# A two-layer graph network on one core: halves of x made anew in each pass, a bias moved to VectorE, new durations in the planner, and two bursts summed in a row in layer 2

## The chip, the cores and the metric

The kernel runs on one core of a Trainium2 chip. The metric is the time of one execution on the device in microseconds (us). TensorE multiplies matrices, VectorE and ScalarE work elementwise, GpSimd here issues indirect DMAs (gathers), and SyncE, ScalarE and GpSimd have DMA queues. In the profile these are PE, DVE, ACT, POOL and SP.

## The reference

Cut to what is computed; N = 6250 nodes, E = 100000 edges, sorted by destination, 256 features, 512 hidden.

```python
def _gin_agg(h, src, dst, eps, n_nodes):
    agg = jax.ops.segment_sum(h[src], dst, num_segments=n_nodes)
    return (1.0 + eps) * h + agg
h = _gin_agg(x, src, dst, eps1, n)            # 6250 x 256
h = jax.nn.relu(h @ W1a + b1a)                # 256 -> 512
h = jax.nn.relu(h @ W1b + b1b)                # 512 -> 512, called h1 below
h = _gin_agg(h, src, dst, eps2, n)            # 6250 x 512
h = jax.nn.relu(h @ W2a + b2a)                # 512 -> 512
out = h @ W2b + b2b                           # 512 -> 256
x = _layernorm(x + out)
```

The destinations are the squares of uniform numbers times 6250, so low nodes have many edges and high nodes few.

## The kernel before, in words

Nodes lie in 49 tiles of 128 (the last has 106). Each layer sums the rows of its table (x in layer 1, h1 in layer 2) over the edges in two ways.

**Light edges** go by gathers. An indirect DMA of GpSimd (`gather`, L450) fetches 128 rows, one edge to a partition. Four of them are a burst, kept in one of six pieces of the buffer `early` (layer 2 has `late` beside it). TensorE sums a burst with four selection matrices `sel` (L942; VectorE makes them at L907), whose result is split (L968 in layer 1; L976 and L978 in layer 2), moved to its rows by a second matmul with `to` (L987; made at L912), and added to the tile's accumulator `acc` on VectorE (L997). A layer has 502 gathers in 126 bursts and 59 groups. The gather that reuses a piece waits for the sum that read it six bursts ago.

**Heavy edges**, those of the first 7 tiles, go by count matrices. VectorE compares numbers with the edges' ends (`ca` L1530, `cb` L1538), TensorE multiplies these into counts (L1576), VectorE adds them into `at` (L1599), ScalarE converts a piece of them (`cf`, L1423), and TensorE multiplies counts by x itself (L1466). For that product x is needed as two parts that add up to it, a rounded one and what the rounding left: its halves, in `xh`. The 7 tiles are taken in four passes, (6,5), (4,3), (2,1) and (0), and each pass goes through all 13 ranges of x (12 of four tiles, one of a single short tile). In the first pass a range of x is loaded (`raw`, L1174), ScalarE makes the rounded half (L1381), VectorE subtracts (L1383), and both halves are written to a DRAM tensor `halves`. The other three passes load the halves from there, and ScalarE rounds both again in place (L1403). Layer 2 reads the saved counts back and multiplies them by halves of h1 (`upper` and `xr`, L1205, L1209, products L1313, added at L1256).

**The dense part** (`dense`) takes up to four tiles whose sums are complete: transposes (L1033), the first weights (L1072), bias and relu on ScalarE (L1082), the second weights (L1103). In layer 1 the second bias comes through TensorE: a matmul (L1102) of a constant `twice` with `first_bias`, a tile holding the bias in two rows as a rounded value and the rest, starts each accumulation. ScalarE then takes the relu from PSUM (L1113) and a DMA on its queue writes h1 (L1114). Layer 2 adds x and the bias (L1121, L1122) and normalises. `first_bias` is made at the start by two small DMAs on ScalarE's queue, a copy on ScalarE and a subtraction on VectorE (L715 to L719), between the check of the inputs (L678, the flag on which the program branches) and the branch.

**The order of the work** is written out by a planner (`Plan`) when the program is built: processes ask for an engine with an assumed duration and a priority, for a buffer (`Room`), or for an event, and the planner hands out the engines in simulated time. What it decides is fixed: each engine runs its instructions in that order and waits for semaphores. Gathers are assumed to take 1.255 us each (`GATHER`), and to land `LANDINGS` later. All of h1 has to be written before layer 2's first gather.

## Time and profile before

| | |
|---|---|
| time, median of 3 runs | 1380.43 us (1375.78 to 1381.38) |
| profiled execution | 1377.27 us, span 1375.3 us, clock 0.964 |
| busy: PE, DVE, ACT, POOL | 1239.8, 832.7, 564.5, 986.1 us |
| DMA | 340.61 MB, mean 248 GB/s |
| halves | 36 loads and 12 writes of 1 MB |

The span is the time from the first to the last instruction of the profiled execution; the execution's own time is 2 us longer. Busy shares are means over the start (checks and tables, to about 31 us), layer 1 (gathers to 671 us), the passage to layer 2 (to 694 us), layer 2 (gathers to 1334 us) and its end. A PE that is busy need not be at its peak, since matmuls overlap.

### The profile page before, as it was taken

To read this page: it belongs to the slowest core of one execution; us is meant where nothing else is said; L and a number is where in the kernel's file an instruction comes from. 1 tells how busy PE (TensorE), PEld (TensorE's weight loads), DVE (VectorE), ACT (ScalarE), POOL (GpSimd) and SP (SyncE) were. 2 spreads that over 40 slices of the span, in tenths; PEclk is the share of its full clock that TensorE was granted. 3 is DMA by queue.
4 is the path that set the end of the run, shared out by engine and by line. 5 is a ranking of instruction groups with operands and counts; after the bars stand their busy time and mean duration, and the time that the engine had idled before them with its cause. 6 is when DMAs were issued, how large, how long until landed. Compare 5 with 4: busy or idle time off the path is not lost.

```text
span 1375.3 us, 18780 instructions
## 1 busy us (share of the span) xinstructions
PE 1239.8 (90%) x6120; PEld 740.1 (54%) x6120; DVE 832.7 (61%) x1940; ACT 564.5 (41%) x977; POOL 986.1 (72%) x1018
## 2 busy tenths in 40 slices
PE   2599999798999999969759999999899999999996
PEld 1245455454554555534426666666566666666666
DVE  7587787576676666401127877687666655655343
ACT  0322477446673675472254433333333323333212
POOL 6677777777777777767367777777777777777760
PEclk9799999899999999989979999999999999999999
DMA  4764489868884888597379888888878989888770
GB/s 105 255 215 143 149 301 330 289 188 275 285 271 155 284 263 274 188 367 226 91 268 325 292 268 261 265 299 268 286 246 302 294 272 307 264 298 253 238 218 30
DMA packets 168188, 340.61 MB, mean 248 GB/s; under 512 B 26108, under 2 KB 74836, under 8 KB 168082
## 3 DMA queue, kind: packets, MB, share of 16 engines
q0 software_dynamic: 64256, 197.46, 45.3%
q1 hardware_dynamic: 81554, 116.23, 25.2%
q10 hardware_dynamic: 22272, 25.63, 5.3%
q8 instruction: 52, 0.85, 0.2%
q14 instruction: 54, 0.44, 0.1%
HBM read 295.99 MB, written 43.24 MB: 247 GB/s over the span
## 4 chain that ended last, share of the span: by engine, by line
PE 57%; DMA 17%; POOL 8%; issue 6%; ACT 4%; DVE 4%; ACTq 0%; DVEq 0%; SPq 0%; POOLq 0%
PE bank L1103 15%; PE bank L1072 12%; PE bank L942 9%; PE bank L1313 7%; POOL early L450 5%; PE bank L987 5%; PE bank L1466 4%; DMA early<-h,srcs 4%; PE bank L1576 3%; POOL late L450 3%; DMA late<-h,srcs 3%; DMA acc<-in_x_dram 3%; PE bank L1033 2%; DMA xh<-halves 2%; PE bank L1102 1%
## 5 line engine op out<-in xcount | busy, mean ns | idle before, releaser
L450 POOL DMA_INDIRECT early<-in_x_dram,srcs x502 | 496.1, 988 | 171.6 <-issue 130.7
L450 POOL DMA_INDIRECT early<-h,srcs x250 | 242.4, 970 | 98.6 <-issue 63.4
L450 POOL DMA_INDIRECT late<-h,srcs x252 | 244.9, 972 | 77.4 <-issue 66.4
L997 DVE SCALAR_TENSOR_TENSOR acc<-bank,mask,acc 128x256 f32<-128x256 f32 (+1 forms) x420 | 247.0, 607 | 78.7 <-PE bank L987 77.5
L1103 PE MATMUL bank<-w1b_s,ht 128*128 128x512 f32 (+1 forms) x392 | 193.7, 619 | 0.0
L1072 PE MATMUL bank<-zt,w2a_s 128*128 128x256 f32 (+2 forms) x864 | 181.6, 364 | 2.2 <-ACT zt L1045 2.2
L942 PE MATMUL bank<-early,sel 128*32 128x256 f32 (+1 forms) x1504 | 152.4, 479 | 23.1 <-DMA early<-h,srcs 12.7
L1072 PEld LDWEIGHTS bank<-zt,w2a_s 128*128 128x128 f32 x864 | 151.8, 192 | 37.1 <-issue 8.4
L1599 DVE TENSOR_TENSOR at<-bank,at 128x490 f32 x173 | 116.1, 671 | 83.8 <-PE bank L1576 33.2
L907 DVE TENSOR_TENSOR sel<-iota,slot 128x256 f32<-128x256 f32 (+2 forms) x118 | 51.7, 438 | 171.2 <-PE bank L942 155.0
L1313 PE MATMUL bank<-upper,cf 128*128 128x512 f32 (+1 forms) x343 | 148.6, 433 | 6.0 <-ACT upper L1205 5.1
L987 PE MATMUL bank<-split,to 128*128 128x256 f32 (+3 forms) x360 | 118.6, 430 | 33.4 <-ACT split L976 9.4
L1313 PE MATMUL bank<-xr,cf 128*128 128x512 f32 (+1 forms) x343 | 137.6, 401 | 0.0
L1466 PE MATMUL bank<-xh,cf 128*128 128x512 f32 (+1 forms) x343 | 114.7, 455 | 10.6 <-ACT xh L1403 10.5
L987 PEld LDWEIGHTS bank<-split,to 128*128 128x128 f32 (+1 forms) x360 | 65.3, 197 | 105.2 <-ACT ht L1082 17.6
L1237 ACT CAST cf<-ci 128x512 fp32r<-128x512 uint16 (+1 forms) x91 | 53.8, 595 | 145.6 <-PE bank L1313 108.4
L1103 PEld LDWEIGHTS bank<-w1b_s,ht 128*128 128x128 f32 (+1 forms) x392 | 71.0, 193 | 69.9 <-issue 65.0
L1072 PE MATMUL bank<-zt,w1a_s 128*128 128x256 f32 (+2 forms) x432 | 99.3, 378 | 4.5 <-ACT zt L1045 3.6
L1103 PE MATMUL bank<-w2b_s,ht 128*128 128x256 f32 (+1 forms) x392 | 102.9, 388 | 0.0
L1538 DVE TENSOR_SCALAR cb<-numbers,spot 128x490 f16<-128x490 f16 x280 | 92.5, 361 | 0.0
L1082 ACT ACTIVATE ht<-bank,b2a_s 128x256 f32<-128x256 f32 (+2 forms) x108 | 44.3, 452 | 116.9 <-PE bank L1072 116.8
L1072 PEld LDWEIGHTS bank<-zt,w1a_s 128*128 128x128 f32 x432 | 79.0, 199 | 22.8 <-ACT zt L1045 7.0
(142 smaller groups left out, 1517.9 us busy)
## 6 DMA issues: line engine op xcount, KB each, us to landing
xh<-halves SPq DMA_DIRECT2D x36, 1024.0 KB
halves<-xh SPq DMA_DIRECT2D x12, 1024.0 KB
h<-h1r ACTq DMA_DIRECT2D x48, 256.0 KB
xr<-h SPq DMA_DIRECT2D x12, 1024.0 KB
counts<-ci ACTq DMA_DIRECT2D x84, 128.0 KB
ci<-counts SPq DMA_DIRECT2D x84, 128.0 KB
acc<-h SPq DMA_DIRECT2D x19, 512.0 KB
early<-in_x_dram,srcs POOLq DMA_INDIRECT x502
```

Of the source, the lines that this page charges most:

```text
L450: nc.gpsimd.indirect_dma_start(out=rows_[:, j, :], out_offset=None, in_=table, in_offset=bass.IndirectOffsetOnAxis(ap=srcs[:, c : c + 1], ...
L907: nc.vector.tensor_tensor(sel[:, :n, :], iota[:, :SLOTS].unsqueeze(1).to_broadcast([P, n, SLOTS]), slot[:, c0 : c0 + n].unsqueeze(2).to_br ...
L942: mm = nc.tensor.matmul(pm[b * SLOTS : (b + 1) * SLOTS], sel[:, c - c0, :], rows_[:, j, :], start=(c == parts[b][0]), stop=(c == parts[b][ ...
L987: nc.tensor.matmul(pu[:, i * width : (i + 1) * width], to[:used], split[:used, l, :], start=(once or l == 0), stop=(once or l == 1),)
L997: nc.vector.scalar_tensor_tensor(acc[t], pu[:, i * width : (i + 1) * width], mask[:, t - lo[g], g : g + 1], acc[t], op0=ALU.mult, op1=ALU.add,
L1072: nc.tensor.matmul(ph[:, (f - o) * TILES * P : (f - o) * TILES * P + nb], wa[:, k, f * P : (f + 1) * P], zt[:, k, :nb], start=(k == 0), st ...
L1103: nc.tensor.matmul(po[:m], ht[:, f, i * P : i * P + m], wb[:, f, :], start=(not once and f == 0), stop=(f == KH - 1),)
L1237: nc.scalar.copy(cf_token.tile[:, :n, :].rearrange("p k j -> p (k j)"), token.tile[:, : n * P],)
L1313: nc.tensor.matmul(bank[token.number][:, :width], cf[:m, j, :], of[:m, j, :], start=(j == 0 and of is upper), stop=(j == len(ks) - 1 and o ...
L1466: nc.tensor.matmul(bank[tokens[i].number][:, : 2 * width], cf[:m, j, :], xh[:m, j, :, :].rearrange("p a d -> p (a d)"), start=(k == 0), st ...
L1538: made = nc.vector.tensor_scalar(token.tile, numbers, spot[:, c : c + 1], None, op0=ALU.is_equal)
L1599: nc.vector.tensor_tensor(to, bank[token.number][:, : NT * W].rearrange("p (k w) -> p k w", w=W), to, op=ALU.add,)
```

## The change

1. `first_bias` and `twice` are gone. A DMA spreads the bias over all partitions into `b1b_s`; VectorE adds it to the second product while taking that from PSUM (L1115 of the new file), and ScalarE takes the relu in SBUF (L1117). `h1r` has three buffers instead of two.
2. `halves` is gone. Each pass loads x itself, and ScalarE and VectorE halve it (L1371, L1373): 52 halvings (48 full, 4 short) instead of 13. `xh` has two buffers instead of three, `raw` two instead of one. The loading begins after 80 us of planned time instead of 20.
3. The planner's assumed durations and priorities differ: elementwise work on VectorE and ScalarE is shorter, a burst's sum is 0.2 plus 0.0021 a column, layer 1's landings take 5 us instead of 3, TensorE gets 0.1 us between two jobs in layer 1, and at most four PSUM banks hold counts (`SIDE`). `cb` has ten buffers instead of nine; its comparisons are ordered two by two.
4. Within a pair of groups layer 2 asks for two bursts together and sums them one behind the other (`JOIN`).

```diff
-LANDINGS = (3.0, 6.0)
+LANDINGS = (5.0, 6.0)
-SUMS = 0.0025
+SUMS = 0.0021
+TURN = 0.2
+JOIN = (1, 2)
+SIDE = 4
 def dve(n):
-    return 0.15 + 0.00105 * n
+    return 0.085 + 0.00105 * n
...
-    twice = const.tile([64, P], F32R, name="twice")
-    nc.vector.tensor_copy(twice, ones[:64].to_broadcast([64, P]))
-    first_bias = const.tile([64, H], F32R, name="first_bias")
-    with tc.tile_pool(name="biases", bufs=1) as biases:
-        whole = biases.tile([64, H], F32, name="whole")
-        nc.vector.memset(whole, 0.0)
-        for k in (0, 32):
-            nc.scalar.dma_start(whole[k : k + 1], b1b.rearrange("(o n) -> o n", o=1))
-        nc.scalar.copy(first_bias, whole)
-        nc.vector.tensor_tensor(
-            first_bias[32:33], whole[32:33], first_bias[32:33], op=ALU.subtract
-        )
+    b1b_s = const.tile([P, H], F32, name="b1b_s")
+    nc.scalar.dma_start(b1b_s, b1b.partition_broadcast(P))
...
+                    for j in range(0, len(todo), n):
+                        some = todo[j : j + n]
+                        for i in some:
+                            yield ("until", selected[pieces[number][i][0]])
+                            yield ("until", arrived[i])
+                        shared = shared or (yield ("get", banks, 0))
+                        yield ("on", "PE", TURN + SUMS * width * len(some), 0)
...
-                        if once and not f:
-                            nc.tensor.matmul(po[:m], twice[:, :m], bias, start=True, stop=False)
...
+                            yield ("on", "DVE", dve(H), 1)
+                            h = h_token.tile
+                            nc.vector.tensor_tensor(h[:m], po[:m], bias[:m], op=ALU.add)
                             yield ("on", "ACT", act(H) + 0.1, 1)
-                            nc.scalar.activation(h[:m], po[:m], AF.Relu)
+                            nc.scalar.activation(h[:m], h[:m], AF.Relu)
...
                 def loading():
+                    yield ("rest", 80.0)
                     for ts, r in turns:
-                        if ts is PASSES[0]:
-                            raw = yield ("get", raw_room, 0)
-                            in_rows(ks, raw.tile, table)
+                        raw = yield ("get", raw_room, 0)
+                        in_rows(ranges[r], raw.tile, table)
                         token = yield ("get", xh_room, 0)
-                        if ts is PASSES[0]:
-                            plan.start(halving(ts, r, xh, raw))
-                        else:
-                            yield ("until", stored[r])
-                            in_rows(
-                                ks, xh.bitcast(F32).rearrange("p k a d -> p k (a d)"),
-                                halves.rearrange("n a d -> n (a d)"),
-                            )
-                            plan.start(rounding(ts, r, xh))
+                        xh_of[ts, r] = token
+                        plan.start(halving(ts, r, token.tile, raw))
...
                         tokens = []
                         for i in some:
-                            tokens.append((yield ("get", banks, 2)))
+                            permit = yield ("get", permits, 0)
+                            tokens.append(((yield ("get", banks, 2)), permit))
```

Where instructions stand now, at three places. In the rows, the name ahead of `<-` is what is written, the rest what is read.

VectorE, near the end of layer 1, before: selection matrices, additions of sums, and the last counts; the halves of this pass come from DRAM.

```order
L1599 TENSOR_TENSOR at<-bank_496,at 128x49x10
L997 SCALAR_TENSOR_TENSOR acc<-bank_494,mask,acc 128x256 x5
L907 TENSOR_TENSOR sel<-iota,slot 128x384
L912 TENSOR_TENSOR to<-iota,home 128x128
L907 TENSOR_TENSOR sel<-iota,slot 128x384
L912 TENSOR_TENSOR to<-iota,home 128x128
L997 SCALAR_TENSOR_TENSOR acc<-bank_496,mask,acc 128x256 x4
```

The same place in the changed kernel, the last pass:

```order
L1373 TENSOR_TENSOR xh<-raw,xh 128x4x256
L1115 TENSOR_TENSOR h1r<-bank_482,b1b_s 128x512
L904 TENSOR_TENSOR sel<-iota,slot 128x384
L909 TENSOR_TENSOR to<-iota,home 128x128
L1373 TENSOR_TENSOR xh<-raw,xh 128x4x256 x2
L1115 TENSOR_TENSOR h1r<-bank_480,b1b_s 128x512
L1373 TENSOR_TENSOR xh<-raw,xh 128x4x256
L1115 TENSOR_TENSOR h1r<-bank_483,b1b_s 128x512
```

Halvings (L1373) and bias additions (L1115) stand between the selection matrices, two halvings one behind the other or behind `to`.

TensorE from the last burst's sum of layer 1 to the last matmul of the layer, before:

```order
L942 MATMUL bank_497<-early,sel 32x256 x16
L987 MATMUL bank_495<-split,to 128x256 x2
L1033 MATMUL bank_493<-ident,acc 128x128 x2
L1033 MATMUL bank_491<-ident,acc 128x128 x2
L1072 MATMUL bank_492<-zt,w1a_s 128x128 x4
L1072 MATMUL bank_496<-zt,w1a_s 128x128 x4
L1072 MATMUL bank_490<-zt,w1a_s 128x128 x4
L1072 MATMUL bank_494<-zt,w1a_s 128x128 x4
L1102 MATMUL bank_497<-first_bias,twice 128x512
L1103 MATMUL bank_497<-w1b_s,ht 128x512 x2
```

The same stretch in the changed kernel, up to its last first-weight matmuls:

```order
L947 MATMUL bank_479<-early,sel 32x256 x4
L1076 MATMUL bank_481<-zt,w1a_s 128x128 x4
L1076 MATMUL bank_485<-zt,w1a_s 128x128 x4
L991 MATMUL bank_483<-split,to 128x256 x2
L1105 MATMUL bank_480<-w1b_s,ht 128x512 x2
L1037 MATMUL bank_478<-ident,acc 128x128 x2
L1105 MATMUL bank_480<-w1b_s,ht 128x512 x2
L1037 MATMUL bank_484<-ident,acc 128x128 x2
L1076 MATMUL bank_482<-zt,w1a_s 128x128 x4
L1076 MATMUL bank_479<-zt,w1a_s 128x128 x4
L1076 MATMUL bank_481<-zt,w1a_s 128x128 x4
L1076 MATMUL bank_485<-zt,w1a_s 128x128 x4
```

Eight first-weight matmuls (L1076) and two pairs of second-weight matmuls (L1105) now stand behind the last sum, ahead of the four rows of L1076 and the eight second-weight matmuls that end the layer in both; the bias matmuls are gone.

TensorE in the last third of layer 2, sums of bursts (L942) among dense work, before:

```order
L942 MATMUL bank_5845<-early,sel 32x512 x4
L987 MATMUL bank_5844<-split,to 128x512 x2
L1072 MATMUL bank_5842<-zt,w2a_s 128x256 x8
L942 MATMUL bank_5845<-late,sel 32x512 x4
L1072 MATMUL bank_5838<-zt,w2a_s 128x256 x8
L942 MATMUL bank_5841<-late,sel 32x512 x4
L987 MATMUL bank_5840<-split,to 128x512 x2
```

And in the changed kernel:

```order
L947 MATMUL bank_5892<-late,sel 32x512 x8
L1037 MATMUL bank_5893<-ident,acc 128x128 x4
L1037 MATMUL bank_5894<-ident,acc 128x128 x4
L1076 MATMUL bank_5891<-zt,w2a_s 128x256 x8
L947 MATMUL bank_5892<-late,sel 32x512 x4
L1076 MATMUL bank_5897<-zt,w2a_s 128x128 x8
L991 MATMUL bank_5896<-split,to 128x512 x2
L1076 MATMUL bank_5895<-zt,w2a_s 128x256 x8
L1076 MATMUL bank_5893<-zt,w2a_s 128x128 x8
L947 MATMUL bank_5894<-early,sel 32x512 x8
```

Where a pair of groups has three bursts or more, two of them (x8) stand together and the odd one (x4) alone; layer 2 has 27 such pairs, none before.

## What I predicted

> **What bounds the kernel now.** I read the page's chain first; it spreads over many lines without naming one. So I took next the gathers of GpSimd in the timeline, from the first to the last of each layer.
>
> ```profile
> span 1375.3 us, 18780 instructions
> 7.57 1.13 POOL L450 DMA_INDIRECT early<-in_x_dram,srcs  x1 [4.30 <-DVE rawf L523]
> ...
> 39.36 1.19 POOL L450 DMA_INDIRECT early<-in_x_dram,srcs  x1 [4.35 <-PE bank L942]
> ...
> 668.85 0.95 POOL L450 DMA_INDIRECT early<-in_x_dram,srcs  x1 [0.30 <-issue]
> 670.10 0.95 POOL L450 DMA_INDIRECT early<-in_x_dram,srcs  x1 [0.30 <-issue]
> 693.72 1.11 POOL L450 DMA_INDIRECT early<-h,srcs  x1 [22.67 <-DMA h<-h1r]
> ...
> 1333.42 0.95 POOL L450 DMA_INDIRECT late<-h,srcs  x1 [0.31 <-issue]
> ```
>
> A line is start, duration, engine, instruction, and in brackets the idle time before it and who ended it. An undisturbed gather comes 1.25 us after the one before (668.85 to 670.10: 0.95 busy, 0.30 of "issue"). A layer has 502 of them; with 1.2527, the mean over undisturbed ones, that is 628.8 us at the least. Layer 1 took from 7.57 to 671.05, 663.5 us, 34.7 over that floor. Layer 2 took from 693.72 to 1334.37, 640.7 us, 11.9 over. Around these lie 7.6 us ahead, 22.7 us from layer 1's last gather to layer 2's first, and 40.9 us behind the last. Every microsecond by which a gather is late in layer 1 moves the rest. So the budget is: what holds up a gather, what lies in the 22.7, and in the 40.9.
>
> Who makes gathers wait, by the view of waits for GpSimd from 60 to 690 us (total, times, longest), and how full the engines are, by windows (busy us):
>
> ```profile
> POOL early L450 <- PE bank L942: 17.0, 21, 3.3
> 60.00:500.00 440.00, 412.98 (x1920) 220.97 (x1921) 316.75 (x710) 230.41 (x381) 335.21 (x339) 0.96 0.74 244
> 700.00:1335.00 635.00, 604.79 (x3121) 396.30 (x3119) 401.83 (x791) 218.55 (x407) 482.46 (x497) 0.98 0.86 280
> ```
>
> The 21 waits for sums contain the usual 0.3 each: 17.0 - 21 x 0.3 = 10.7 us of real waiting. TensorE is 94% busy in the first stretch (412.98 of 440) and 95% in layer 2 (604.79 of 635), so it is never far from being the limit itself. VectorE stands at 72% (316.75 of 440).
>
> **A gather is also held by VectorE.** This decides the forecast, so its rows come first: gathers beside instructions with two SBUF operands (the halving's subtraction, L1383: first, one in the middle, last, and one that began after the gather), then one beside an addition from PSUM (L1256).
>
> ```profile
> 57.70 1.22 DVE L1383 TENSOR_TENSOR xh<-raw,xh 128x1024 fp32r<-128x1024 f32 x1
> 58.73 1.00 POOL L450 DMA_INDIRECT early<-in_x_dram,srcs  x1 [0.30 <-issue]
> ...
> 171.63 0.95 POOL L450 DMA_INDIRECT early<-in_x_dram,srcs  x1 [0.30 <-issue]
> 171.73 1.22 DVE L1383 TENSOR_TENSOR xh<-raw,xh 128x1024 fp32r<-128x1024 f32 x1
> ...
> 222.48 1.22 DVE L1383 TENSOR_TENSOR xh<-raw,xh 128x1024 fp32r<-128x1024 f32 x1
> 222.54 1.98 POOL L450 DMA_INDIRECT early<-in_x_dram,srcs  x1 [0.30 <-issue]
> ...
> 270.30 0.43 DVE L1383 TENSOR_TENSOR xh<-raw,xh 106x256 fp32r<-106x256 f32 x1 [6.93 <-ACT xh L1381]
> 270.36 1.19 POOL L450 DMA_INDIRECT early<-in_x_dram,srcs  x1 [0.30 <-issue]
> ...
> 1141.55 0.69 DVE L1256 TENSOR_TENSOR acc<-bank,acc 128x512 f32<-128x512 f32 x1 [0.88 <-PE bank L1313]
> 1141.91 0.95 POOL L450 DMA_INDIRECT late<-h,srcs  x1 [0.30 <-issue]
> ```
>
> The gather at 222.54 starts inside the subtraction and lasts 1.98 us: 0.95 counted from 0.13 before the subtraction's end at 223.70. The one at 171.63 had started before the subtraction and shows nothing. Of the 13 subtractions, 57.70 to 270.30, eleven lengthened a gather, by 6.5 us together, or 0.52 for each of the 12 full ones. The addition with one operand in PSUM holds nothing (0.95), and I found the same at all 239 gathers that start within L997, L1256 or L1599, which read PSUM. The Trainium skill ("SBUF — State Buffer", section "Who interferes with whom") says that a VectorE instruction with two SBUF inputs contends with a GpSimd instruction that reads SBUF, and one with a single SBUF input doesn't; by that rule the trace agrees (1.98 against 0.95 us).
>
> **1. Start (first_bias gone): -4.1 us.**
>
> ```profile
> 30.93 0.14 DVE L678 CAST flag<-fsum 1x1 int32<-1x1 f32 x1
> 36.57 0.68 DVE L719 TENSOR_TENSOR first_bias<-whole,first_bias 1x512 fp32r<-1x512 f32 x1 [4.86 <-ACT first_bias L718]
> 37.31 0.36 DVE L907 TENSOR_TENSOR sel<-iota,slot 128x192 f32<-128x192 f32 x1
> 38.02 1.92 PE L942 MATMUL bank<-early,sel 128*32 128x256 f32 x12 [7.33 <-ACTq L1889]
> ...
> 40.85 2.55 POOL L450 DMA_INDIRECT early<-in_x_dram,srcs  x1 [0.30 <-issue]
> 43.70 2.22 POOL L450 DMA_INDIRECT early<-in_x_dram,srcs  x1 [0.30 <-issue]
> ```
>
> The flag of the input check is there at 31.07. VectorE then waits 4.86 us for the rounded bias, subtracts, and only at 37.31 makes the first selection matrix that TensorE's first sum (38.02) needs; the gather at 39.36 waits for that sum, 4.35 us instead of 0.30. The removed instructions stand in this chain alone, so the selection matrix moves up by 37.31 - 31.07 less a branch of about 1 us (estimate), some 5 us, more than the stall of 4.05. Bounds: 0 (another first wait, for weights or for the branch) to -7 (the two slow gathers behind it, at 40.85 and 43.70, 2.55 + 2.22 - 2 x 0.95 = 2.9 us too long, go as well). I take -4.1.
>
> **2. Halves made anew in each of four passes: +18.7 us on GpSimd.** Groups of the trace (line, engine, operation, count | busy us, mean ns):
>
> ```profile
> L1383 DVE TENSOR_TENSOR xh<-raw,xh 128x1024 fp32r<-128x1024 f32 x12 | 14.6, 1217 | 1.1 <-ACT xh L1381 1.1
> L1381 ACT CAST xh<-raw 128x1024 fp32r<-128x1024 f32 x12 | 12.6, 1046 | 1.8 <-ACT ci L1431 0.9 <-DMA raw<-in_x_dram 0.5 <-ACT h1r L1113 0.4
> L1403 ACT CAST xh<-xh 128x2048 fp32r<-128x2048 f32 x36 | 68.2, 1897 | 8.3 <-DMA xh<-halves 5.0 <-ACT ci L1431 2.9 <-ACT h1r L1113 0.4
> L1102 PE MATMUL bank<-first_bias,twice 64*128 64x512 f32 x48 | 24.7, 515 | 0.6 <-DVE at L1599 0.5
> L1256 DVE TENSOR_TENSOR acc<-bank,acc 128x512 f32<-128x512 f32 x84 | 57.7, 687 | 45.8 <-PE bank L1313 45.6
> ```
>
> Added are 36 full subtractions of 1.217 us (43.8 us of VectorE) and 3 short ones. They have two SBUF operands, and a subtraction of 1.22 us nearly always contains the start of a gather, since one starts each 1.25 us. At 0.52 us a piece that is 36 x 0.52 = 18.7 us that gathers come later, less what a gather would have waited for TensorE anyway (part 3). Low end: 14, where a quarter fall beside such waits. High end: 26, since in the new order some subtractions stand directly behind each other or behind the selection matrices' instructions, and a gather is held through all of them, as at 222.54. The same section of the Trainium skill infers that descriptor generation isn't stalled by such a subtraction; the row at 222.54 speaks against it, and by that inference this term would be 0 (a rival below). Everything else in this part costs nothing: ScalarE does 36 x 1.05 more for the copies and 36 x 1.90 less for the rounding, 31 us less in all, and isn't at its limit. The halves' traffic shrinks (12 writes and 36 reads of 1 MB go, 36 reads of 0.5 MB come), but no gather is late for a landing in the view of waits beyond the usual 0.3, so I put the smaller traffic at 0, with -2 as its gain at most.
>
> **3. TensorE's share of layer 1: -8 us.** The 49 bias matmuls go. A row says 515 ns each; they overlap their neighbours, and by start to start (682.04 to 682.46, below) it is 0.42, so 49 x 0.42 = 21 us of work. With the later start of the products (80 us instead of 20) and shorter assumed durations, less work stands ahead of the sums in the middle of the layer. That can remove at most the 10.7 us of waits; I take 8, since the last few sums keep their neighbours. Worst: +5, if the plan, which still counts 1.255 us a gather where part 2 makes it 1.29 on average ((628.8 + 18.7) / 502), lines sums up too early, and TensorE stands in front of them. The addition that replaces the matmul reads PSUM, so it holds no gather; it costs VectorE 49 x 0.69 = 34 us by L1256, which with part 2 makes 78 us more in layer 1. In the stretch from 60 to 500 that fills part of 123 us of idle time; this cover is what rival B takes away.
>
> **4. The passage between the layers: +3.7 us.**
>
> ```profile
> 674.81 1.13 PE L987 MATMUL bank<-split,to 128*128 128x256 f32 x4 [0.72 <-ACT split L968]
> 676.05 1.66 DVE L997 SCALAR_TENSOR_TENSOR acc<-bank,mask,acc 128x256 f32<-128x256 f32 x4 [14.19 <-PE bank L987]
> 677.37 0.83 PE L1033 MATMUL bank<-ident,acc 128*128 128x128 f32 x4 [1.43 <-DVE acc L997]
> 678.27 3.84 PE L1072 MATMUL bank<-zt,w1a_s 128*128 128x128 f32 x32
> 682.04 0.49 PE L1102 MATMUL bank<-first_bias,twice 64*128 64x512 f32 x1
> 682.46 1.98 PE L1103 MATMUL bank<-w1b_s,ht 128*128 128x512 f32 x4
> ```
>
> Nothing covers this chain: the last sum, its merge (674.81), the additions (676.05), transposes, first weights (678.27), second weights, the relu, and h1's write, on which layer 2's first gather waits. In the new order eight first-weight matmuls of other tiles (0.24 each by 678.27, whose 32 instructions are 16 matmuls) stand between sum and merge, where TensorE used to idle 0.72: +1.2. A pair of second-weight matmuls (1.98 by 682.46) stands between merge and transposes, where it idled 1.43 for the additions: +0.5; another between the transposes: +1.9. Two bias matmuls go (-0.9); the addition and its hand-over come (0.69 + about 0.3): +1.0. Sum +3.7; between 0 (if TensorE is through with that work before the last burst lands, in another place than the order has it) and +6.
>
> **5. Layer 2 sums two bursts in a row: -6.5 us.**
>
> ```profile
> 654.75 0.64 PE L942 MATMUL bank<-early,sel 128*32 128x256 f32 x8
> 657.23 1.07 PE L942 MATMUL bank<-early,sel 128*32 128x256 f32 x16
> ...
> 1299.39 1.06 PE L942 MATMUL bank<-late,sel 128*32 128x512 f32 x8
> ```
>
> One burst of 256 columns takes 0.64 (8 instructions), two in a row 1.07 and not 1.28: 0.21 saved where one follows the other. At 512 columns a burst takes 1.06, and no row shows two in a row; I use the same 0.21. The new order has 27 such pairs: 27 x 0.21 = 5.7 us of TensorE, 95% busy there, so it appears in what is left behind the last gather. With 0.8 for a better packed end, -6.5. Bounds: -12 (the order leaves less behind the last burst) to +2 (a pair waits for its second burst and frees the first one's buffer 5 us later). Gathers of layer 2 keep their 12 us over the floor, as its two-operand instructions stay.
>
> **The sum.** -4.1 + 18.7 - 8 + 3.7 - 6.5 = +3.8 us. The profiled execution took 1377.27 (span 1375.3), so 1381.1 on its scale; it lies 3.2 below the median of the runs shown, and I add half of that: **1383 us**, against 1380.43 before. About 0.5%, 6.9 us, is what a measurement of this kernel can tell from no change, so this is "same".
>
> **Rivals.**
> A, faster: TensorE, not GpSimd, sets layer 1. For it: 94% busy, waits for sums throughout. Then held gathers are partly covered and the bias work counts. All 10.7 us of waits and the 2.9 us of slow gathers at the start go, half of the holds are covered (9.4): -4.1 - 10.7 - 2.9 + 9.4 + 3.7 - 6.5 = -11.1, **1368**. Against: between the waits, gathers run at 1.25 for long stretches. Chance 0.28.
> A', faster: the section's inference above is right for most of the new subtractions: 1383 - 18.7 = **1364**. Against it stand eleven lengthened gathers. Chance 0.05.
> B, slower: VectorE becomes the limit of layer 1. It runs in order; behind a subtraction that waits for its load or for ScalarE's copy stand the selection matrices, the additions and the counts that TensorE waits for. It decides from about 85% in 60 to 500: 316.75 plus two thirds of 78 is 369 of 440, 84%. Then part 3 gives +5 instead of -8 and the holds reach 26: -4.1 + 26 + 5 + 3.7 - 6.5 = +24.1, **1403**. Against: VectorE's idle time in the trace is mostly its own waiting, not others' waiting for it. Chance 0.17.
> C: joining does nothing, since the pair's wait eats it, and TensorE's tail stays: **1390**. Chance 0.10.
> The forecast keeps 0.40, spread over 1374 to 1392.
>
> **How the numbers follow.** Faster by over 0.5% is below 1373.5: A and A' and a little of the forecast, 0.34. Slower is above 1387.3: B, most of C, a fifth of the forecast, 0.34. Same: 0.32. Both outer cases are near, so the range goes from 1362 (A' with a little of its bounds) to 1403 (B); the forecast's own is 1374 to 1392.
>
> **What would show it.** Right: no wait over 1 us of the first gathers; gathers under the new subtractions of 1.2 to 2 us, some 45 lengthened by 23 to 27 us together; layer 1's gathers ending near 678; waits for sums under 3 us in all; a passage of 26 to 27; and less than 37 us behind the last gather. Wrong: lengthened gathers adding under 15 us, or gathers ending layer 1 before 668 (A); VectorE over 88% busy with TensorE waiting for selection matrices or additions (B).

## The result, and the profile after

The changed kernel takes 1389.55 us (median of 20 runs, 1380.11 to 1398.87), the kernel before 1378.32 (20 runs): 1.0085 times as long, 95% interval 1.0063 to 1.0108. A second set of 12 runs gave 1385.78 against 1378.42, 1.0050 (1.0023 to 1.0077). So it is slower, by 0.5 to 0.85%. I had forecast 1383 and called that "same", with "slower" from 1387.3 on, in a range of 1362 to 1403; the first set lies just above that line, the second just below. (Of the experiments below, eight ran in two sessions in which the kernel before took 1627 us and the gathers paused for some 2 us at about every eighth; a ratio from those sessions is compared only with others of the same session.)

The gathers of the changed kernel, as shown of before, with the first sum and the selection matrix ahead of it:

```profile
span 1387.6 us, 18666 instructions
8.76 1.13 POOL L458 DMA_INDIRECT early<-in_x_dram,srcs  x1 [5.49 <-DVE rawf L531]
...
32.12 0.14 DVE L686 CAST flag<-fsum 1x1 int32<-1x1 f32 x1
33.09 0.36 DVE L904 TENSOR_TENSOR sel<-iota,slot 128x192 f32<-128x192 f32 x1 [0.84 <-DVE flag L686]
33.79 1.92 PE L947 MATMUL bank<-early,sel 128*32 128x256 f32 x12 [1.91 <-DVE to L909]
35.26 1.13 POOL L458 DMA_INDIRECT early<-in_x_dram,srcs  x1 [0.31 <-DMA early<-in_x_dram,srcs]
...
675.38 0.95 POOL L458 DMA_INDIRECT early<-in_x_dram,srcs  x1 [0.30 <-issue]
705.07 0.97 POOL L458 DMA_INDIRECT early<-h,srcs  x1 [28.74 <-issue]
...
1350.38 0.95 POOL L458 DMA_INDIRECT late<-h,srcs  x1 [0.31 <-issue]
```

The gather at 35.26 no longer waits (0.31 instead of 4.35 at 39.36): VectorE goes from the flag (32.12) straight to the selection matrix (33.09). Layer 1's last gather still starts later than before, 675.38 against 670.10; layer 2's first comes 28.7 us after that one's end instead of 22.7.

Waits of GpSimd for sums from 60 to 690 us, and the engines by windows (busy us of PE, PEld, DVE, ACT, POOL):

```profile
POOL early L458 <- PE bank L947: 3.4, 11, 0.3
```

```profile
60.00:500.00 440.00, 380.84 (x1875) 212.85 (x1872) 360.11 (x782) 220.37 (x387) 339.10 (x332) 0.95 0.62 190
700.00:1335.00 635.00, 592.80 (x3033) 395.18 (x3032) 397.58 (x783) 224.11 (x414) 473.94 (x489) 0.96 0.85 275
```

Eleven waits of the usual 0.3: nothing is left of the 10.7 us. TensorE's share from 60 to 500 fell from 94% to 87%, VectorE's rose from 72% to 82%. The group of the halvings' subtraction, and the gather that one of them held longest:

```profile
L1373 DVE TENSOR_TENSOR xh<-raw,xh 128x1024 fp32r<-128x1024 f32 x48 | 58.7, 1222 | 29.0 <-ACT xh L1371 29.0
```

```profile
234.49 2.05 POOL L458 DMA_INDIRECT early<-in_x_dram,srcs  x1 [0.30 <-PE bank L1550]
234.50 1.21 DVE L1373 TENSOR_TENSOR xh<-raw,xh 128x1024 fp32r<-128x1024 f32 x1
```

A gather that starts with the subtraction lasts 2.05 us instead of 0.95. I added up, gather by gather, what lies over 0.95 us (lengthening), what lies over 0.31 between two gathers (waits), and the rest of the execution, for six executions:

| us | before | changed | changed, again | bias only | short halving | halves kept |
|---|---|---|---|---|---|---|
| first gather starts | 7.6 | 8.8 | 9.3 | 9.4 | 9.6 | 9.4 |
| layer 1's gathers | 663.5 | 667.6 | 670.8 | 652.0 | 659.4 | 664.3 |
| - lengthening in it | 20.7 | 38.0 | 42.5 | 22.2 | 29.7 | 23.5 |
| - of that under the halving | 6.5 | 20.2 | 24.3 | 7.6 | 7.2 | 5.0 |
| - waits in it | 14.6 | 1.0 | 0.6 | 1.9 | 1.7 | 13.1 |
| passage | 22.7 | 28.7 | 27.8 | 26.9 | 29.2 | 31.4 |
| layer 2's gathers | 640.7 | 646.3 | 639.4 | 637.7 | 642.2 | 642.7 |
| behind the last gather | 41.0 | 36.3 | 36.5 | 42.4 | 37.8 | 38.1 |
| span | 1375.3 | 1387.6 | 1383.8 | 1368.4 | 1378.2 | 1385.8 |

The last four columns are runs described below; one execution each. Executions of one kernel lie up to 19 us apart (1380.11 to 1398.87), so a difference of a few us between two columns can be that of the executions.

### The profile page after: what moved, and what is told of

Same layout as the page of the kernel before. It is cut to its first block, busy times and chain, and to the rows that moved or that the text cites. A ratio compares the mean times of both kernels' runs of the same rounds, so it can differ in the third digit from the quotient of the medians.

```text
span 1387.6 us, 18666 instructions
## 1 busy us (share of the span) xinstructions
PE 1216.1 (88%) x6071; PEld 746.2 (54%) x6071; DVE 898.7 (65%) x2025; ACT 533.2 (38%) x976; POOL 1002.8 (72%) x1018
## 4 chain that ended last, share of the span: by engine, by line
PE 52%; DMA 14%; POOL 10%; issue 10%; DVE 6%; ACT 4%; ACTq 0%; DVEq 0%; SPq 0%; POOLq 0%
PE bank L1076 12%; PE bank L1105 11%; PE bank L947 10%; PE bank L1317 10%; POOL early L458 9%; DMA early<-in_x_dram,srcs 6%; PE bank L991 4%; DMA acc<-h 4%; PE bank L1550 2%; PE bank L1436 2%; DVE at L1573 2%; PE bank L1037 2%; DMA late<-h,srcs 2%; POOL late L458 1%; DMA early<-h,srcs 1%
## 5 line engine op out<-in xcount | busy, mean ns | idle before, releaser
L458 POOL DMA_INDIRECT early<-in_x_dram,srcs x502 | 513.9, 1024 | 159.2 <-issue 128.9
L1001 DVE SCALAR_TENSOR_TENSOR acc<-bank,mask,acc 128x256 f32<-128x256 f32 (+1 forms) x420 | 242.4, 606 | 30.2 <-PE bank L991 30.1
L1105 PE MATMUL bank<-w1b_s,ht 128*128 128x512 f32 (+1 forms) x392 | 186.5, 604 | 0.0
L1076 PE MATMUL bank<-zt,w2a_s 128*128 128x256 f32 (+2 forms) x864 | 181.8, 364 | 0.6 <-ACT zt L1049 0.5
L1076 PEld LDWEIGHTS bank<-zt,w2a_s 128*128 128x128 f32 x864 | 151.6, 191 | 38.2 <-issue 11.7
L1573 DVE TENSOR_TENSOR at<-bank,at 128x490 f32 x173 | 115.3, 667 | 22.3 <-ACT cf L1394 13.3
L947 PEld LDWEIGHTS bank<-early,sel 128*32 128x32 f32 x1504 | 33.0, 110 | 149.7 <-issue 109.4
L1105 PEld LDWEIGHTS bank<-w1b_s,ht 128*128 128x128 f32 (+1 forms) x392 | 73.8, 193 | 67.9 <-issue 59.9
L982 DVE TENSOR_TENSOR split<-bank,split 128x512 fp32r<-128x512 f32 (+1 forms) x90 | 61.8, 687 | 74.5 <-ACT split L980 74.5
L1076 PE MATMUL bank<-zt,w1a_s 128*128 128x256 f32 (+2 forms) x432 | 103.9, 390 | 3.6 <-ACT zt L1049 2.5
L1436 PE MATMUL bank<-xh,cf 128*128 128x512 f32 (+1 forms) x343 | 102.4, 437 | 5.0 <-DVE xh L1373 3.8
L1105 PE MATMUL bank<-w2b_s,ht 128*128 128x256 f32 (+1 forms) x392 | 103.1, 390 | 0.0
L1511 DVE TENSOR_SCALAR cb<-numbers,spot 128x490 f16<-128x490 f16 x280 | 88.2, 355 | 21.8 <-PE bank L1550 21.7
```

What stands on the lines that cost most here:

```text
L458: nc.gpsimd.indirect_dma_start(out=rows_[:, j, :], out_offset=None, in_=table, in_offset=bass.IndirectOffsetOnAxis(ap=srcs[:, c : c + 1], ...
L947: mm = nc.tensor.matmul(pm[b * SLOTS : (b + 1) * SLOTS], sel[:, c - groups[g][0], :], rows_[:, l, :], start=(c == part[0]), stop=(c == par ...
L982: nc.vector.tensor_tensor(split[:used, 1, :], ap[:used], split[:used, 0, :], op=ALU.subtract)
L1001: nc.vector.scalar_tensor_tensor(acc[t], pu[:, i * width : (i + 1) * width], mask[:, t - lo[g], g : g + 1], acc[t], op0=ALU.mult, op1=ALU.add,
L1076: nc.tensor.matmul(ph[:, (f - o) * TILES * P : (f - o) * TILES * P + nb], wa[:, k, f * P : (f + 1) * P], zt[:, k, :nb], start=(k == 0), st ...
L1105: nc.tensor.matmul(po[:m], ht[:, f, i * P : i * P + m], wb[:, f, :], start=(f == 0), stop=(f == KH - 1),)
```

## The experiments

Theory 1 is the prediction's: what the change loses is time in which the new subtractions hold gathers, more than the start and the waits give back. Theory 2, its rival: the planner's new order loses it (the passage, layer 2, waits that move), and the holds are covered. "Holds" and "lengthening" are used alike below.

**The halving with one SBUF operand** (three runs). The subtraction is replaced at its place, so that the planner's order is the same to the instruction; the second half of x is zero, or x's first half times 0.00001, so the outputs lack the precision that it gives.

```diff
-nc.vector.tensor_tensor(xh[:m, js, 1, :], raw.tile[:m, js, :], xh[:m, js, 0, :], op=ALU.subtract)
+nc.vector.tensor_scalar(xh[:m, js, 1, :], xh[:m, js, 0, :], 0.0, None, op0=ALU.mult)
```

Expected:

> The changed kernel with the halving's subtraction replaced by a multiplication by zero with one SBUF operand, at the same place in the order: the second half of x is left out (zeros), the rest is computed. Theory 1 (two SBUF operands hold gathers): gathers lengthened at this line fall from 20.2 us to under 2, layer 1's gathers end 12 to 20 us earlier, the time is 1370 to 1379 us, below the kernel before or equal to it. Theory 2 (the planner's new order is what costs): the holds are covered by other waits, the time stays at 1386 to 1392. If the one-operand form holds gathers too, they stay lengthened and so does the time.

It ran in a session at 1627 us: 0.9950 times the kernel before (0.9915 to 0.9985). The instruction took 0.72 us, not 1.22; lengthening under it was 5.1 us and not under 2, 23 of 52 held a gather. The unaltered changed kernel wasn't in that session. So the factor became a scalar for each partition (`lneps[:m, 0:1]`), to make it slower:

> The changed kernel with the subtraction replaced by a multiplication with one SBUF tensor and a scalar per partition of 0.00001, at the same place in the order, meant to last the 1.2 us of the subtraction (the form with a constant took 0.72): the second half of x is left out but for that factor. Theory 1 (two SBUF operands hold gathers): gathers lengthened at this line fall from 20.2 us to under 2, and the time is 10 to 16 us below the changed kernel in this call. Theory 2 (order): within 3 us of it. If what counts is that VectorE is busy, not how many operands it reads, it is also within 3 us.

This ran beside the changed kernel: 1374.74 us against 1385.78, 0.9984 times the kernel before (0.9963 to 1.0005) against 1.0050: 11.0 us less. Its instruction in the groups, and the gathers beside two of them:

```profile
L1373 DVE TENSOR_SCALAR xh<-xh,lneps 128x1024 fp32r<-128x1024 f32 x48 | 37.3, 776 | 32.9 <-ACT xh L1371 32.9
```

```profile
356.67 0.74 DVE L1373 TENSOR_SCALAR xh<-xh,lneps 128x1024 fp32r<-128x1024 f32 x1
356.78 1.45 POOL L458 DMA_INDIRECT early<-in_x_dram,srcs  x1 [0.30 <-PE bank L1076]
...
632.32 0.75 DVE L1373 TENSOR_SCALAR xh<-xh,lneps 128x1024 fp32r<-128x1024 f32 x1 [3.34 <-ACT xh L1371]
632.84 1.05 POOL L458 DMA_INDIRECT early<-in_x_dram,srcs  x1 [0.30 <-issue]
```

It again took 0.78, and it still held gathers, by 7.2 us together: 1.45 where one starts with it, 1.05 near its end. So the expectation of under 2 us missed, and "one operand is free" is wrong for this form. The size is right all the same: lengthening falls from 42.5 to 29.7 us, by 12.8, and layer 1's gathers take 11.4 us less, which is the whole gain of 11.0. Theory 2 asked for a difference within 3 us. (Under the halving itself 17.1 us went; 4.3 came back under other instructions. What of it is due to the second operand and what to the shorter time isn't separated.) VectorE is also 21 us less busy here (58.7 to 37.3 us), but the gathers' waits didn't shrink (0.6 to 1.7), so that is not how the time was won. Last, the same with a stride of two elements:

> The changed kernel with the subtraction replaced by a multiplication with one SBUF tensor, read and written with a stride of two elements so that it lasts about 1.2 us (the contiguous form took 0.78 and still lengthened gathers by 7.2 us); the second half of x is left out but for a factor of 0.00001. If what holds a gather is the second SBUF operand or a fast mode: lengthening at this line under 2 us and 12 to 18 us below the changed kernel, 0.992 to 0.997 times the kernel before. If any VectorE instruction of 1.2 us between SBUF tensors holds a gather: lengthening of 17 to 25 us and the changed kernel's 1.005 to 1.0085. If gathers are free but VectorE's own time is the limit: under 2 us of lengthening, yet 1.002 or more.

Inconclusive: in the 1627 session it came to 0.9993 (0.9955 to 1.0031), and the instruction took 0.77 us even so, with 7.0 us of lengthening. A one-operand instruction of 1.2 us was not had.

**The bias part alone**, made on the kernel before: `first_bias`, `twice` and L1102 go, `b1b_s` and the addition come, nothing else.

```diff
-                        if once and not f:
-                            nc.tensor.matmul(po[:m], twice[:, :m], bias, start=True, stop=False)
...
+                            yield ("on", "DVE", dve(H), 1)
+                            nc.vector.tensor_tensor(h[:m], po[:m], bias[:m], op=ALU.add)
```

> The kernel before with the bias part alone: no first_bias at the start, no bias matmuls, VectorE adds the bias ahead of the relu, planned with the old durations. Theory 1: the start's 4.05 us of waiting goes, waits for sums shrink by up to 8 us, the passage stays within 1 us, holds stay at 15 us: 6 to 12 us below the kernel before (0.991 to 0.996). If TensorE's work doesn't matter: only the start, 4 us (0.997). If the addition on VectorE delays what TensorE waits for: equal or above (1.0 to 1.005).

1374.27 against 1378.42 us, 0.9962 (0.9942 to 0.9981): the fastest complete kernel of this study, but 4.2 us and not the 6 to 12 of theory 1. The number alone can't tell theory 1 from "only the start" (0.997); the trace can. Layer 1's gathers and the passage in it:

```profile
9.40 1.12 POOL L450 DMA_INDIRECT early<-in_x_dram,srcs  x1 [6.13 <-DVE rawf L523]
...
660.45 0.95 POOL L450 DMA_INDIRECT early<-in_x_dram,srcs  x1 [0.30 <-issue]
662.23 3.70 PE L1091 MATMUL bank<-w1b_s,ht 128*128 128x512 f32 x8
665.86 1.93 PE L932 MATMUL bank<-early,sel 128*32 128x256 f32 x32
688.30 1.19 POOL L450 DMA_INDIRECT early<-h,srcs  x1 [26.90 <-DMA h<-h1r]
```

From 9.40 to 661.40 are 652.0 us, 11.5 less than before: waits fell from 14.6, the start's 4.05 among them, to 1.9, and lengthening rose by 1.5. So part 1 and the gain of part 3 come from the bias alone, planned with the old durations. It gives 4.2 us of that back in the passage (26.9), which theory 1 had expected within 1 us: in its order, too, second-weight matmuls (662.23, 3.70 us) stand ahead of layer 1's last four sums (665.86). Beside the run with the shorter halving (1374.74 us) the two are alike: with the holds reduced, the rest of the change shows no gain over the bias part.

**Halves kept in DRAM**, all else as changed (three buffers `xh`, one `raw`, nine `cb`), made twice.

```diff
+        halves = odram.tile([N, 2, D], F32, name="halves")
-                        raw = yield ("get", raw_room, 0)
-                        in_rows(ranges[r], raw.tile, table)
+                        if ts is PASSES[0]:
+                            raw = yield ("get", raw_room, 0)
+                            in_rows(ks, raw.tile, table)
...
+                            plan.start(rounding(ts, r, xh))
```

> The changed kernel with the halves written to DRAM once and read back in three passes, as in the kernel before (three xh buffers, one raw, nine cb), all else as changed, planned anew. Theory 1: 36 subtractions fewer, holds at this line back to about 6 us, waits for sums of 0 to 5 us, time 1373 to 1381. Theory 2: the other parts cost the 11 us, time 1386 to 1394.

In the 1627 session: 1.0124 (1.0082 to 1.0167), from six runs that spread from 1622.53 to 1651.68 us. Again, beside the changed kernel:

> The changed kernel with the halves written to DRAM once and read back in three passes, as in the kernel before, all else as changed; the same kernel as the second run. Theory 1: 8 to 15 us below the changed kernel of this call, holds at this line near 6 us. Theory 2: within 4 us of the changed kernel. If the traffic of 30 MB counts (as the second run, 1.0124 times the kernel before on its chip, suggests): above the changed kernel.

1385.13 us, 1.0045 (1.0027 to 1.0064), the changed kernel beside it 1.0050: by the number, theory 2. Its trace shows a wait that neither theory had. ScalarE, TensorE and GpSimd in its first 65 us:

```profile
55.04 1.04 ACT L1386 CAST xh<-raw 128x1024 fp32r<-128x1024 f32 x1 [18.77 <-DMA raw<-in_x_dram]
55.99 5.00 ACT L881 ACTIVATE acc<-acc,e 128x512 f32<-128x512 f32 x8
60.89 0.62 ACT L978 COPY split<-bank 64x256 f32<-64x256 f32 x2
61.30 2.37 PE L992 MATMUL bank<-split,to 64*128 64x256 f32 x4 [18.97 <-ACT split L978]
...
64.98 1.01 POOL L458 DMA_INDIRECT early<-in_x_dram,srcs  x1 [11.34 <-PE bank L948]
```

My version plans the first load after 20 us instead of 80, so ScalarE stands before that load for 18.77 us, with the scalings and the split behind it; TensorE waits 18.97 us for the split and a gather 11.34 for TensorE. That one wait is 0.8% of the time, and no other kernel of this table has it. Without it the run would stand near 0.9965, theory 1's place; lengthening is back at 23.5 us as expected. That subtraction is an argument, not a run. The run for it, the first load after 80 us:

> The kernel with the halves kept in DRAM and all else as changed once more, its first load planned after 80 us as in the changed kernel instead of 20, which put ScalarE before a late load at the start and made one gather wait 11.0 us. Theory 1: without that wait, 0.8% below that run: 0.994 to 0.999 times the kernel before, and holds at the halving near 5 us. Theory 2 (the rest of the change costs): 1.003 or more.

It fell in a 1627 session, 1.0062 (1.0027 to 1.0097). The wait at the start is gone there. By the lines set for it the number is theory 2's (1.003 or more); those lines were drawn for a chip on which the kernel before takes 1380 us, and the changed kernel wasn't beside it. So whether DRAM halves with the rest of the change beat the kernel before stays open, and theory 1 has no support from these three runs but the lengthening of 23.5 us.

**Joining, and layer 2's loads.** `JOIN = (1, 1)`, twice, and a planner that counts 15 us instead of 6 from an accumulator's load to its scaling in layer 2:

```diff
-JOIN = (1, 2)
+JOIN = (1, 1)
```

```diff
-                yield ("rest", LOAD)
+                yield ("rest", LOAD if once else 15.0)
```

> The changed kernel with each burst of layer 2 summed alone (JOIN of 1 and 1); layer 1 is unchanged. If joining saves its 0.2 us a pair (27 pairs, 5.7 us) and TensorE bounds layer 2: 1393 to 1397. If joined pairs make layer 2's new waits (7.2 us at 1188 to 1210): 1380 to 1386. If it does neither: 1387 to 1392.

> The changed kernel in which the planner of layer 2 assumes 15 us instead of 6 from an accumulator's load to its scaling on ScalarE (the trace shows 14.8 and 15.2); layer 1 is unchanged. If layer 2's loss is ScalarE standing before a late load with the split behind it: TensorE's waits for the split fall from 23.8 to under 10 us, gathers wait under 2 us instead of 7.2, time 1380 to 1385. If TensorE is full anyway and the waits only move: 1387 to 1392.

> The changed kernel with each burst of layer 2 summed alone, as in the third run, on a chip on which the kernel before takes 1380. Joining saves TensorE 5.7 us, and layer 2 gets that much longer without it: 1.009 to 1.012 times the kernel before. If joined pairs cause as much waiting as they save: 1.004 to 1.008, as the changed kernel. If they cost: under 1.003.

Without joining 1.0057 (1.0028 to 1.0087) in the first 1627 session and 1.0037 (1.0002 to 1.0072) in the second; with the loads counted at 15 us 0.9998 (0.9971 to 1.0025) in the first. The changed kernel itself ran in neither, so none of the three tells what joining gives; that is open.

**The changed kernel again**, the measure used above:

> The changed kernel once more, unaltered, as the measure for the runs beside it, since the first four ran on a chip on which the kernel before took 1627 us. On a chip on which the kernel before takes about 1380 us: 1.006 to 1.011 times the kernel before. On a chip like that of the first four, where GpSimd also waits for things that are not the program's: 0.995 to 1.01.

1.0050 (1.0023 to 1.0077), a little under the range given.

**All that seemed to help** (halves kept and loaded late, loads of layer 2 at 15 us):

> The kernel with halves kept in DRAM and loaded late (the second of this call), with the planner of layer 2 counting 15 us from an accumulator's load to its scaling. What the runs so far add up to: start -4, waits -9, holds as before, passage +4 to +6, layer 2 -6 to 0: 0.990 to 0.996 times the kernel before, below both kernels. If layer 2's waits move elsewhere: as the second of this call.

In the 1627 session 1.0034 (0.9995 to 1.0073) and not 0.990 to 0.996, beside 1.0062 without the 15 us: no proof of anything below both kernels. What the runs show to beat both is the bias part alone.

## Why the prediction was right or wrong

**Start and waits (parts 1 and 3), forecast -12.1 us: right.** Waits fell from 14.6 to 1.0 and 0.6, by 13.6 and 14.0. The start's 4.05 went to the last tenth, the two slow gathers behind it stayed, and the worst case, a plan that puts TensorE in front of sums, didn't come. The run with the bias alone shows the cause. The slow gathers were never part of this chain; they lie beside VectorE's clearing of `at`:

```profile
36.56 1.58 DVE L1520 MEMSET at<- 128x1827 uint32 x1 [0.33 <-DVE to L909]
36.69 2.55 POOL L458 DMA_INDIRECT early<-in_x_dram,srcs  x1 [0.30 <-issue]
```

Of the seven such memsets of the changed trace three stand beside a gather of 2.55 to 2.79 us, and the other four beside gathers of 0.95; why these three was not tried.

**Holds (part 2), forecast +18.7: right.** All lengthening in layer 1 grew by 17.3 and 21.8 us, that under the halving by 13.7 and 17.8, to 20.2 and 24.3 (my sign was 23 to 27); for each of the 48 full subtractions that is 0.42 and 0.51 us, where I had used 0.52. The run with the shorter instruction shows that it costs what it adds up to: 12.8 us of lengthening less, 11.0 us of time less. Back-to-back subtractions didn't reach the high end. Rival A (covered by TensorE) falls with that run; rival B (VectorE as the limit) didn't come either: VectorE was at 82%, near the 84% reckoned, yet gathers waited 1.0 us in layer 1 where B needed more waits than before, and TensorE from 60 to 680 us waited most for landings of gathers (39.0 us of 81.7, against 24.9 for VectorE). The line of 85% that B was given was my choice; no run shows from where VectorE would be the limit. The sums' waits for gathers and for VectorE:

```profile
PE bank L947 <- DMA early<-in_x_dram,srcs: 39.0, 24, 4.6
PE bank L947 <- DVE at L1573: 5.8, 8, 2.4
```

Rival A', which I took from the inference in the Trainium skill ("SBUF — State Buffer", section "Who interferes with whom"), falls with the 20.2 and 24.3 us under the halving.

**The passage (part 4), forecast +3.7: under-sized.** It cost 6.1 and 5.1, just over and just under what I had as bound, 6. The work counted behind the last sum is there; what I had put at nothing is the lag ahead of it. The last sum before, and then the changed kernel:

```profile
673.45 0.64 PE L942 MATMUL bank<-early,sel 128*32 128x256 f32 x8 [2.33 <-DMA early<-in_x_dram,srcs]
```

```profile
676.74 0.64 PE L947 MATMUL bank<-early,sel 128*32 128x256 f32 x8
677.31 5.42 PE L1105 MATMUL bank<-w1b_s,ht 128*128 128x512 f32 x12
682.66 0.64 PE L947 MATMUL bank<-early,sel 128*32 128x256 f32 x8
685.21 1.13 PE L991 MATMUL bank<-split,to 128*128 128x256 f32 x4
688.11 1.88 PE L1105 MATMUL bank<-w1b_s,ht 128*128 128x512 f32 x4
693.62 7.03 PE L1105 MATMUL bank<-w1b_s,ht 128*128 128x512 f32 x16
```

Six second-weight matmuls (677.31, 5.42 us) stand between the last two sums, so the last sum starts 6.3 us after the last gather's end; before it was 2.4 (673.45 against 671.05). That is +3.9, and +3.0 in the second execution; the rest of the chain, which I had put at +3.7, took 2.1 more in both. So the term came out small by one thing left out and one counted too high. The order of both kernels was there to read; I counted only from the last sum on.

**Layer 2 (part 5), forecast -6.5: wrong in one execution, nearly right in the other.** From layer 2's first gather to the end it was 681.6 us before, 682.5 and 675.9 after: +0.9 and -5.7. The part behind the last gather shrank by 4.7 and 4.5. What ate it in the first is time that I had excluded by "Gathers of layer 2 keep their 12 us over the floor" (they had 17.5 and 10.6), part of it in this wait:

```profile
1173.73 0.83 ACT L1086 ACTIVATE ht<-bank,b2a_s 128x256 f32<-128x256 f32 x2
1180.78 1.15 ACT L880 ACTIVATE acc<-acc,e 128x1024 f32<-128x1024 f32 x1 [6.22 <-DMA acc<-h]
1181.84 0.57 ACT L980 CAST split<-bank 128x512 fp32r<-128x512 f32 x1
1182.45 1.52 PE L991 MATMUL bank<-split,to 128*128 128x512 f32 x2 [6.35 <-ACT split L980]
1183.77 0.63 PE L1317 MATMUL bank<-upper,cf 128*128 128x512 f32 x1
...
1186.07 0.40 PE L1317 MATMUL bank<-upper,cf 128*128 128x512 f32 x1
1186.63 1.92 PE L947 MATMUL bank<-late,sel 128*32 128x512 f32 x16
1188.00 0.95 POOL L458 DMA_INDIRECT late<-h,srcs  x1 [5.30 <-PE bank L947]
```

ScalarE stands before the load of an accumulator for 6.22 us, the split (1181.84) behind it, TensorE behind the split (6.35), the pair of sums behind that, and the gather at 1188.00 waits 5.30. The failed step is that quoted sentence: I took TensorE's saved time as shown whole behind the last gather and didn't ask what the planner's order does to ScalarE there, which waits longer for accumulators' loads in layer 2, before, after, and after again (total, times, longest):

```profile
ACT acc L883 <- DMA acc<-h: 30.0, 11, 8.4
```

```profile
ACT acc L880 <- DMA acc<-h: 48.3, 13, 9.9
```

```profile
ACT acc L880 <- DMA acc<-h: 47.5, 12, 10.6
```

ScalarE waits as long in the second execution, yet there the gathers waited 2.2 us in layer 2, against 7.2 in the first and 0.6 before; so these waits alone don't make the loss. I also left out TensorE's clock. Behind the wait of 6.35 us the same product takes 0.63 us at 1183.77 and 0.40 at 1186.07, and the windows show the granted clock (the third number from the end) at about half of it and back:

```profile
1183.00:1186.00 3.00, 3.00 (x8) 2.30 (x8) 1.54 (x3) 0.14 (x1) 0.00 (x0) 0.54 0.41 137
1186.00:1190.00 4.00, 4.00 (x26) 1.96 (x26) 2.00 (x4) 1.21 (x2) 1.69 (x2) 1.00 0.21 49
```

Added up over layer 2 and the end, each busy stretch of TensorE weighted with the clock granted in it:

| us | before | changed | changed, again |
|---|---|---|---|
| busy, as if at full clock | 628.4 | 621.0 | 621.8 |
| busy time lost to a lower clock | 11.0 | 16.4 | 14.9 |
| idle | 42.3 | 45.2 | 39.2 |

So TensorE's work did shrink by about the 6.5 us forecast (7.4 and 6.6; the two other executions with the changed layer 2, short halving and halves kept, have 621.0 and 620.6, the bias alone 628.0), and a lower clock took 5.4 and 3.9 of it back. Idle time makes most of the difference between the two executions (+2.9 and -3.1). That the order makes the waits and the waits the lower clock is argued and not shown, and what of the shrinking is joining's stays open. The pair itself (1186.63, 16 instructions) takes 1.92 where two single sums take 2.12: 0.2 us in this pair.

**A term that was missing.** The first gather starts at 8.8 to 9.7 us in every kernel with `b1b_s` and at 7.57 in the one trace of before. That is 1.2 to 2.1 us; I counted nothing there. Whether the spread load of the bias, queued early, delays the first tables was not tried.

Together: the forecast for the profiled span was +3.8 us; the spans gave +12.3 and +8.5, the medians +11.2 and +7.4. The size was off by layer 2, the passage and the first gather, all to the slow side; the two large terms, of 12 down and 19 up, were right. Little of this cancelled: layer 1's gathers took +4.1 and +7.4 us where the terms for it add up to +6.6, and the other errors are nearly all to the slow side. In layer 2 the nearly right number of the second execution is partly luck, since less idle time there made good what the lower clock took.

## What to carry to other kernels

Where GpSimd issues gathers in an unbroken row, count a VectorE instruction with two SBUF operands not only in VectorE's time but also on GpSimd's chain, here with a third to nearly a half of its length (0.42 to 0.52 us of 1.22). Look for a form with one operand in PSUM. Doing it once and keeping the result took the lengthening back to 23.5 us here, but no run shows a lower time for it. In a chain at the end of a stage, count TensorE's queue from the last piece of data that arrives, not from the last instruction that is needed. When a plan's durations change, look at the in-order engine with idle time, here ScalarE: a late load at its head stops what stands behind it (18.77 us in the kernel with halves kept).

## What the runs showed of the hardware

I looked at gathers that start inside a VectorE instruction, at least 0.25 us before its end, in the second execution of the changed kernel. With two SBUF operands 37 of 39 were held under the subtraction, 18 of 20 under L1502 (`ca`), 8 of 9 under L1126 (layer 2's bias). With an operand in PSUM none of 90 was held under L1001 (`acc`), none of 49 under L1573 (`at`), none of 11 under the new bias addition (L1115). New to me was the third kind: one SBUF operand. Under L1148 (normalising, 128x256 in 0.42 us) 1 of 9 was held, by 0.13 us; under L1511 (`cb`, 128x490, fp16, 0.36 us) 6 of 17, by 0.18 us at most; under the replacement in its own trace (128x1024 in 0.78 us) 14 of 15, by up to 0.51. The replacement differs from L1148 in speed: from its 106x256 form (0.42 us) to 128x1024 it takes 0.47 ns more for each element of a row, the subtraction 1.04 (0.42 to 1.22 us), about twice as much. The Trainium skill ("SBUF — State Buffer", section "Who interferes with whom") says that VectorE's two-port fast modes, which a tensor_scalar can enter, keep GpSimd out as well; by that rule the trace agrees. What the same section of the Trainium skill says of one SBUF input holds outside these modes only, a condition that my sentence in the prediction left out.

The sessions at 1627 us: one place there, from the second run without joining, on three engines.

```profile
1110.75 0.69 DVE L1260 TENSOR_TENSOR acc<-bank,acc 128x512 f32<-128x512 f32 x1 [1.38 <-remote]
1110.75 0.62 ACT L1241 CAST cf<-ci 128x512 fp32r<-128x512 uint16 x1 [6.73 <-remote]
...
1114.98 0.79 PE L991 MATMUL bank<-split,to 128*128 128x512 f32 x1 [1.14 <-issue]
```

VectorE and ScalarE resume together at 1110.75, released by no instruction that the profile shows ("remote"); TensorE shows idle time in "issue". GpSimd's waits come to 90 to 147 us a layer there, against 0.6 to 14.6 in the executions of the table. The cause was not tried.
